# Three early loads on another queue, and the count of rows to redo one row block later

## The chip, the cores and the metric

The kernel runs on one core of a Trainium2 chip. The core has five engines with a queue of their own each: PE (TensorE, matrix products and transposes), DVE (VectorE), ACT (ScalarE), POOL (GpSimd) and SP (SyncE, which issues DMAs). Each queue is worked off in order, and the engines wait for each other through semaphores. The metric is the time of one execution on the device in microseconds.

## The reference, cut to what matters

Two layers on 4096 nodes with 256 features. The first is graph attention with 4 heads, the second a diffusion of two steps, in which a dense attention keeps of each row only the largest probabilities, up to a sum of 0.9.

```python
h = relu(layernorm(x));  x = x + layer0(h, adj, W, a, gamma, beta)
h = relu(layernorm(x));  x = x + layer1(h, adj, W1, W2, W3, U1, U2, ln_g, ln_b)

# layer 0: g = h @ W, 4 heads of 64
src, dst = g . a[:64], g . a[64:]
e = leaky_relu(src[i] + dst[j], 0.2), only where adj[i, j] > 0
out = layernorm(softmax(e) @ g)

# layer 1
R = adj + I, rows divided by their sums
for n in range(2):
    P = softmax((Xa W1^T W2^T)(Xa W3^T)^T)
    A = P, each row cut to its largest entries whose sum reaches 0.9, then rescaled
    Xf = R @ Xf;  Xa = A @ Xa
    Z += Xf @ U1[n]^T + Xa @ U2[n]^T
return layernorm(X + Z)
```

## The kernel before, in words

The 4096 rows are 32 blocks of 128 rows (NB = 32, P = 128); the rows stay in the SBUF tile X. All work stands in stretches under `tc.manual_schedule`: the order of the instructions on each engine is the order in which the program writes them. Loops that would have to be interleaved are written as generators, or as functions that are called between pieces of another loop. DMAs take their semaphores from a set of eight lanes in turn; a DMA that takes a lane again first waits until the one before it on that lane has landed.

The beginning. Block 0 of the rows is loaded by SP (L197), then blocks 1 to 3 in one DMA (L201), then the other 28 blocks in seven DMAs of four blocks (`block_rows`, L195). ACT's queue loads the logits' vector `a_r`, copied to all partitions (L198), the weights in two halves `wx` (L200), and then three small weights of the second layer (L204 to L206). DVE begins with `measured(0)`, the moments of block 0 (L149, L150). Then, for each half k of the weights, it multiplies `wx` with the two halves of `a_r` and adds up (L571, L573, twice each); after k = 0 it takes the moments of blocks 1 to 3, after k = 1 those of blocks 4 to 7. POOL turns moments into scales (`steps`, L141 to L144), ACT normalizes a block (`opened`, L240), PE transposes it (L247) and multiplies it with the weights (L254), and then ACT, DVE and POOL form the weighted rows in three bf16 parts (`turn_of`, once per block). After that PE does the sums over neighbours for 16 passes (L395), and the first hop of the diffusion (L622).

The attention. Step n of the two works through the row blocks b with `attend`. In it there are eight groups g of four columns each: `turn(r, g + 1)` transposes four pieces of the masked exponentials on PE into a PSUM tile `tp` (L1088; there are two such tiles, used in turn) and ACT copies it out to `eT` (L1090); `gather(r, eT[g], g, cur)` multiplies it with the rows (L1096, four matmuls). A dictionary `between` names functions that are called at the end of group g. After the last group come `contributed` (L1106), `weighed` (L1110) and `scaled` (L1101); in the very last block of the last step the first two stand in group 4. `chosen_kept(b)` is DVE's part for a block: it finds the threshold, masks the exponentials (L1022), and carries earlier blocks on through `finish` (L1274 or L1277), `finish_scale` (L1284, L1285), `gathered` (L1114 to L1116), `normal` (L1292), `polished` (L1296 to L1298) and `finish_rows` (L1302 to L1304).

The repair. Rows whose threshold is not certain must be redone. `last_chosen`, called in group 5 of block 30, ends with the tables `undone` and `failed` (`questioned`, L1164 to L1176). `looked`, called in group 6 of block 30, sums them: `counted` calls `totals` twice (PE matmul L878 into a `tp` tile; DVE L880, L882 and L884 read it), and `chosen` makes the list of blocks to redo (DVE, L1192 to L1201). `number` loads the sum into a register of every engine (L1187), and after the last block `repaired` branches on it (L1264). In this run the count is zero and the branch is not taken. In the first step block 31 also prepares the next hop: `both_weights` loads 512 KB of weights (L717), `begin` loads four row blocks and four adjacency rows (L455, L474), `split` and `own` work on these (L461, L462, L482).

Of the kernel before, what the change touches and what calls it, by code (L numbers as in the profile page):

```python
# [26 lines left out]
P = 128  # L27
# [29 lines left out]
def gat_then_top_p_diffusion(  # L57
# [18 lines left out]
    nc = tc.nc  # L76
    N, D = x.shape
    HD = a.shape[0] // 2
    H = D // HD
    DA = w2_t.shape[0]  # L80
    NB = N // P
# [80 lines left out]
    with tc.tile_pool(name="l0", bufs=1) as l0, tc.tile_pool(name="l0s", bufs=2) as l0s, tc.tile_pool(name="l0o", bufs=1) as l0o:  # L162
# [26 lines left out]
        with tc.manual_schedule(engines=every | {ET.SP}):  # L189
            wx = rp.tile([P, KC, D + 2 * H], F32, name="wx", tag="ar", bufs=4)  # L190
            a_r, w1_s, w2_s, w1_r, sT = (rp.tile(sh, F32, name=x, tag="hl", bufs=5) for x, sh in (
                ("a_r", [P, 2 * HD]), ("w1_s", [P, KC, DA]), ("w2_s", [DA, DA]), ("w1_r", [DA, KC, P]), ("sT", [P, P])))
# [2 lines left out]
                nc.sync.dma_start(X[:, ts(g, 4), :], x[ts(g, 4 * P), :].rearrange("(b p) d -> p b d", p=P))  # L195

            nc.sync.dma_start(X[:, 0, :], x[:P, :])  # L197
            nc.scalar.dma_start(a_r, bass.AP(tensor=a.tensor, offset=a.offset, ap=[[0, P], [1, 2 * HD]]))  # L198
            for k in range(KC):
                nc.scalar.dma_start(wx[:, k, :D], w[ts(k, P), :])  # L200
            nc.sync.dma_start(X[:, 1:4, :], x[P:4 * P, :].rearrange("(b p) d -> p b d", p=P))  # L201
            for g in range(1, NB // 4):
                block_rows(g)
# [237 lines left out]
        S = SimpleNamespace(spare=None)  # L441
# [6 lines left out]
        def source(A, n):  # L448
            if n in A.src or n >= len(order):
                return  # L450
            if A.hop == 0:
                A.src[n] = X[:, order[n][1], :]
            else:
                A.src[n] = S.rows.tile([P, D], F32, name="x1", bufs=3) if n % 5 < 3 else S.rows.tile([P, D], F32, name="xa")
                nc.sync.dma_start(A.src[n], xf_d[order[n][1]])  # L455

        def split(A, n):
            while A.parted < min(n, len(order)):
                src = A.src[A.parted]
                hl = rp.tile([P, 2, D], F32R, name="hl", bufs=5)  # L460
                nc.scalar.copy(hl[:, 0, :], src)  # L461
                nc.vector.tensor_tensor(hl[:, 1, :], src, hl[:, 0, :].bitcast(F32), ALU.subtract)  # L462
                A.hl[A.parted] = hl
                A.parted += 1

        def edge(A, n):
            if n in A.ar or n >= len(order):
                return
            p, j = order[n]
            if S.spare is not None and n % 5 == 4:  # L470
                ar = S.spare.tile([P, G0 * P], F32R, name="aru", tag="u")
            else:
                ar = rp.tile([P, G0 * P], F32R, name="ar", bufs=4)
            nc.sync.dma_start(ar.bitcast(F32), adj_d[p, :, j, :].bitcast(F32))  # L474
            A.ar[n] = ar

        def own(A, n):
            while A.owned < min(n, len(order)):
                p, j = order[A.owned]
                if j // G0 == p:  # L480
                    block_ = A.ar[A.owned][:, ts(j % G0, P)]
                    nc.vector.tensor_tensor(block_, block_.bitcast(F32), ident, ALU.add)  # L482
                A.owned += 1
# [171 lines left out]
        def begin(A, n):  # L655
            for i in range(n):
                source(A, i)
                edge(A, i)
            A.begun = n
# [53 lines left out]
    def both_weights():  # L713

        u2 = l1e.tile([P, N + NB], F32, name="u2", tag="e1")[:, :KC * STEPS * D].rearrange("p (k n m) -> p k n m", k=KC, n=STEPS)
        for i in range(STEPS):
            nc.sync.dma_start(u2[:, :, i, :], u2_t[i].rearrange("(k p) m -> p k m", p=P))  # L717
        S.u2 = [u2]
# [150 lines left out]
    def table(name):  # L869
        return small.tile([P, NB], F32, name=name, bufs=1)  # L870

    def col(name, bufs=None):
        return small.tile([P, 1], F32, name=name, bufs=bufs or 4)
# [312 lines left out]
    def number(R, total):  # L1186
        return nc.values_load(total[1], engines=everyone, min_val=0, max_val=6 * P * NB)  # L1187
# [93 lines left out]
    def finish_scale(r):  # L1281
        if r.n + 1 == STEPS:
            r.rs = col("rs")
            nc.gpsimd.tensor_scalar(r.rs, r.mv[:, :, 1], EPS, None, ALU.add)  # L1284
            nc.gpsimd.tensor_tensor(r.rs, r.rs, mhalf, ALU.pow)  # L1285
            if getattr(r, "eased", False):
                r.nmr = col("nmr")
                nc.gpsimd.tensor_scalar(r.nmr, r.mv[:, :, 0], r.rs, -1.0, ALU.mult, ALU.mult)
# [58 lines left out]
    for n in range(STEPS):  # L1347
        cur = X
        G = SimpleNamespace()
        found = [table(f"found{i}") for i in range(3)]  # L1350
        blocks = {}
        with tc.manual_schedule(engines=every):
            pieces = first_hop if n == 0 else hops(second)
            filling, picking = fills(n, G, found, blocks), picks(n, found, blocks)
            done = 0 if n else NB - G0 - LOOK
            for i, _ in enumerate(pieces, 2 * done):
                if n > 0 and i % 6 == 1 and i // 6 < NB // 4:
                    g = i // 6
                    nc.sync.dma_start(cur[:, ts(g, 4), :], xa_d[ts(g, 4)].rearrange("b p d -> p b d"))
                if (n == 0 or i > 10) and i // 2 % NB != NB - 2:  # L1360
                    next(filling, None)
                    if i // 2 % NB < NB - 3 or i % (2 * NB) == 2 * NB - 1:
                        next(picking, None)
                if i == 2 * len(order) - 6:
                    first = turn(blocks[0], 0)
            weights(n)
            for _ in filling:
                next(picking, None)
            for _ in picking:
                pass  # L1370

            def chosen_kept(b):

                r = blocks[b]
                if not hasattr(r, "kept"):
                    candidates(r, found)
                if b > 2:
                    polished(blocks.pop(b - 3))
                if b + 1 < NB and not hasattr(blocks[b + 1], "thirded"):
                    third_probe(blocks[b + 1])  # L1380
                if b > 1:
                    finish(blocks[b - 2])
                    finish_scale(blocks[b - 2])
                if b + 2 < NB and not hasattr(blocks[b + 2], "stepped"):
                    first_step(blocks[b + 2])
                if 0 < b < NB - 1:
                    gathered(blocks[b - 1])
                if not hasattr(r, "kept"):
                    masked(r)
                if 1 < b < NB - 1:  # L1390
                    normal(blocks[b - 2])

            R = SimpleNamespace(n=n, kT=G.kT, qT=G.qT, nm=G.nm, table=found[0])

            def last_chosen():
                chosen_kept(NB - 1)
                R.failed, R.undone = questioned(G, found)

            def looked():
                counted(R)  # L1400
                chosen(R)

            def beginning():
                normal(blocks[NB - 3])
                gathered(blocks[NB - 2])
                finish(blocks[NB - 2])
                finish_scale(blocks[NB - 2])
                R.count = number(R, R.undone)

            beside = {NB - 2: {5: last_chosen, 6: looked}, 0: dict(zip((0, 1, 3, 5, 6), S.turned))}  # L1410
            for b in range(NB - 1):
                chosen_kept(b)
                if b + AHEAD < NB:
                    blocks[b + AHEAD] = began(n, b + AHEAD, G)
                attend(blocks[b], cur, blocks.get(b + AHEAD),
                       beside.get(b, {}), [first] if b == 0 else ())
            r = blocks[NB - 1]

            def earlier():
                polished(blocks[NB - 3])  # L1420
                finish_rows(blocks[NB - 2])

            beside = {0: beginning, 3: earlier}
            if n + 1 < STEPS:
                second = hop_of(n + 1)
                beside.update({1: both_weights, 2: lambda: begin(second, 4), 5: lambda: split(second, 2), 6: lambda: (split(second, 4), own(second, 4))})
            attend(r, cur, None, beside)
            for m in range(second.begun if n + 1 < STEPS else 0):
                for s in range(KC):
                    graph_products(second, m, s, (0,))  # L1430
            finish(r)
            finish_scale(r)
            finish_rows(r)
        repaired(R, cur)
# [32 lines left out]
```

## Time and profile before

| what | value |
|---|---|
| median of 3 runs | 2867.93 us (2864.26 to 2868.86) |
| the profiled execution, its time | 2866.9 us |
| its span in the profile | 2865.1 us |
| TensorE clock granted, mean | 0.995 of full speed |
| PE busy | 2795.3 us, 98% of the span |
| DVE busy | 2169.1 us, 76% |
| ACT busy | 1918.8 us, 67% |
| POOL busy | 865.7 us, 30% |
| the beginning, up to PE's first neighbour sum | some 88 us |
| first step, block 31 and step end | about 1779 to 1811 us |
| last step, block 31 and the end | about 2838 to 2865 us |

Busy time is the time in which an engine had an instruction in work; issuing DMAs and loading registers do not count. The profile shows one execution, so its durations are compared with its own time of 2866.9 us, of which 1.8 us lie outside the span. In a timeline each line gives start and duration in us, the engine, the line of the code, the operation, its output and input, and how many instructions are merged into it; brackets give the time that the engine stood idle before it and what ended that. SPq and ACTq stand for DMA issues of those queues.

### The profile page before, as it was taken

Reading aid. Unit: us, or ns where it says so; the run is one execution under the profiler, and the core shown is the slowest. Engines: PE = TensorE matmul, PEld = TensorE weight load, DVE = VectorE, ACT = ScalarE, POOL = GpSimd, SP = SyncE. Lnnn points to the kernel's source line nnn. Section 1 sums busy time; section 2 is a strip of 40 time slices with the busy share of each in tenths; the row PEclk is TensorE's granted clock in tenths of the full one; section 3 lists DMA queues with packets and bytes.
Section 4 is the critical chain, followed back from the end, with each engine's and each line's share of the span. In section 5 each row is a group of like instructions: output and inputs, shape, how many; then the busy total and the mean of one; then the engine's idle time right before and its main releaser. Section 6 shows DMA issues by size and latency. Waiting matters only on the chain. (4 is left out here: it accounts for less than half of the span.)

```text
span 2865.1 us, 51492 instructions
## 1 busy us (share of the span) xinstructions
PE 2795.3 (98%) x18777; PEld 2436.3 (85%) x18777; DVE 2169.1 (76%) x5069; ACT 1918.8 (67%) x3065; POOL 865.7 (30%) x1811
## 2 busy tenths in 40 slices
PE   5999999999999999999999999999999999999998
PEld 4899999999978788888888888667778888888886
DVE  8867868678554385888888887333665999999996
ACT  7876886879543636788878874233627788777882
POOL 6402121010000121222332231000204756666664
PEclk8999999999999999999999999999999999999999
DMA  8969596696376783000000001767991111111110
GB/s 192 243 250 204 204 234 188 229 198 222 133 236 196 240 298 95 20 20 20 27 20 20 20 20 56 229 200 236 327 340 43 31 41 31 31 31 33 39 29 25
DMA packets 190394, 376.48 MB, mean 131 GB/s; under 512 B 18224, under 2 KB 143152, under 8 KB 186032
## 3 DMA queue, kind: packets, MB, share of 16 engines
q1 hardware_dynamic: 146832, 275.05, 29.9%
q0 software_dynamic: 21504, 83.89, 12.3%
q10 hardware_dynamic: 21792, 14.11, 1.6%
q8 instruction: 152, 2.49, 0.4%
q14 instruction: 114, 0.93, 0.1%
HBM read 305.55 MB, written 113.57 MB: 146 GB/s over the span
## 5 line engine op out<-in xcount | busy, mean ns | idle before, releaser
L1096 PE MATMUL acc<-X,eT 128*128 128x256 f32 x4096 | 973.6, 383 | 3.4 <-ACT eT L1090 2.8
L1096 PEld LDWEIGHTS acc<-X,eT 128*128 128x128 f32 x4096 | 739.1, 190 | 111.5 <-ACT eT L1090 31.5
L395 PE MATMUL acc<-ut,m 128*128 128x195 bf16 (+1 forms) x8192 | 698.7, 246 | 2.2 <-DVE st L412 1.7
L395 PEld LDWEIGHTS <-m 128*128 128x128 fp8e4 x8192 | 695.9, 97 | 4.9 <-DVE st L412 2.2
L369 ACT ACTIVATE g<-sr,d_big 128x1024 uint8<-128x1024 f32 x448 | 472.6, 1136 | 3.4 <-DVE m L375 3.4
L911 ACT ACTIVATE e<-mm,nm 128x1024 f32<-128x1024 f32 x256 | 286.1, 1117 | 200.1 <-PE mm L728 198.8
L1090 ACT COPY eT<-tp 128x512 f32<-128x512 f32 x512 | 296.5, 580 | 87.5 <-PE tp L1088 87.4
L997 DVE MAX8 cand<-big 128x8 f32<-128x228 f32 (+1 forms) x1152 | 348.2, 380 | 0.0
L622 PE MATMUL mm<-ar,hl 128*128 128x512 f32 x844 | 340.7, 407 | 5.9 <-ACT ob L502 1.3
L979 DVE SCALAR_TENSOR_TENSOR big<-e,c 128x4096 f32<-128x4096 f32 x58 | 261.9, 4516 | 97.5 <-POOL c L964 67.1
L622 PE MATMUL acc<-ar,hl 128*128 128x512 f32 x844 | 328.6, 392 | 2.3 <-DVE stage L632 1.3
L935 POOL TENSOR_TENSOR sums<-sums 128x2 f32<-128x2 f32 x64 | 12.6, 197 | 1030.9 <-ACT void L918 1030.9
L1088 PE MATMUL tp<-ident,e 128*128 128x128 f32 x2048 | 306.0, 272 | 0.8 <-DVE e L1022 0.8
L1088 PEld LDWEIGHTS tp<-ident,e 128*128 128x128 f32 x2048 | 254.8, 140 | 60.2 <-PE acc L1106 1.2
L375 DVE TENSOR_TENSOR m<-g,ax 128x512 uint32<-128x512 uint32 x256 | 180.8, 706 | 109.9 <-PE acc L395 91.4
L1022 DVE SCALAR_TENSOR_TENSOR e<-e,found 128x4096 f32<-128x4096 f32 x58 | 259.1, 4468 | 0.0
L918 ACT ACTIVATE void<-e,c1x 128x2048 int8<-128x2048 f32 x128 | 257.4, 2011 | 0.8 <-ACT stage L651 0.8
L918 ACT ACTIVATE void<-e,c 128x2048 int8<-128x2048 f32 x128 | 257.5, 2012 | 0.0
L728 PE MATMUL mm<-kT,qT 128*128 128x512 f32 x512 | 198.4, 468 | 2.9 <-ACT e L911 1.9
L376 DVE TENSOR_TENSOR m<-m,ax 128x512 uint32<-128x512 uint32 x256 | 180.4, 705 | 26.0 <-PE acc L395 0.9
L622 PEld LDWEIGHTS mm<-ar,hl 128*128 128x128 f32 x844 | 158.6, 188 | 44.9 <-issue 5.0
L622 PEld LDWEIGHTS acc<-ar,hl 128*128 128x128 f32 x844 | 158.6, 188 | 39.9 <-issue 4.9
(302 smaller groups left out, 3507.4 us busy)
## 6 DMA issues: line engine op xcount, KB each, us to landing
ar<-adj_d SPq DMA_DIRECT2D x211, 512.0 KB, 4.7
adj_d<-ax POOLq DMA_DIRECT2D x32, 2048.0 KB, 7.7
ut<-uv_d SPq DMA_DIRECT2D x60, 784.0 KB, 5.6
aru<-adj_d SPq DMA_DIRECT2D x45, 512.0 KB, 4.6
ax<-in_adj_t_dram POOLq DMA_DIRECT2D x32, 512.0 KB, 17.4
x<-xf_d SPq DMA_DIRECT2D x78, 128.0 KB, 4.9
xf<-xft_d SPq DMA_DIRECT2D x64, 128.0 KB, 2.3
sr<-s_d SPq DMA_DIRECT2D x15, 512.0 KB, 4.9
```

Source lines behind the costliest of these rows:

```text
L369: nc.scalar.activation(g[:, c, :], shared[k].sr, AF.Relu, scale=BIG, bias=d_big[:, h, j:j + 1])
L395: nc.tensor.matmul(shared[k].acc[i][:, t, :cols], m[t][:, c, ts(i, P)], shared[k].ut[j // QUARTER][:, j % QUARTER, t, :cols], start=(j == ...
L622: nc.tensor.matmul(A.acc[c][s], A.hl[m][:, t, ts(s, P)], A.ar[m][:, ts(c, 512)], start=(j == 0 and t == 0), stop=(j == NB - 1 and t == 1))
L728: nc.tensor.matmul(pm[:, h, :], q[t], kT[:, ds(h * (N // 2) + c * 512, 512)], start=(t == 0), stop=(t == 1))
L911: nc.scalar.activation(ev[:, :, c, :], r.pm[c], AF.Exp, bias=r.nm, accum_out=r.sums[:, c // 2, c % 2:c % 2 + 1])
L918: nc.scalar.activation(void, r.e[:, ts(h, N // 2)], (AF.Relu, AF.Sign)[i], bias=r.c1, scale=-1.0, accum_out=r.sums[:, h, 2 + i:3 + i])
L979: nc.vector.scalar_tensor_tensor(big, r.e, r.c3, r.e, ALU.is_le, ALU.mult, accum_out=r.low3)
L997: nc.vector.max(cand[:, s, :], big[:, edges[s]:edges[s + 1]])
L1022: nc.vector.scalar_tensor_tensor(r.e, r.e, r.t, r.e, ALU.is_ge, ALU.mult, accum_out=kept)
L1088: nc.tensor.transpose(pt[:, i, :], r.e[:, ts(4 * g + i, P)], ident)
L1090: nc.scalar.copy(eT, pt)
L1096: nc.tensor.matmul(r.acc[:, 0, :], eT[:, i, :], cur[:, j, :], start=(j == 0), stop=(j == NB - 1))
```

## The change

The loads of `a_r` and of the two halves of `wx` are issued by SP instead of ACT, at the same place in the program: behind block 0 and ahead of blocks 1 to 3. In the attention, `looked` is called in group 1 of block 31 instead of group 6 of block 30. The load of the count into registers leaves `beginning` (group 0 of block 31) and becomes a function `asked`, called in group 4. In the first step `both_weights` goes from group 1 to group 2, ahead of `begin`. No computation is added or left out.

```diff
             nc.sync.dma_start(X[:, 0, :], x[:P, :])
-            nc.scalar.dma_start(a_r, bass.AP(tensor=a.tensor, offset=a.offset, ap=[[0, P], [1, 2 * HD]]))
+            nc.sync.dma_start(a_r, bass.AP(tensor=a.tensor, offset=a.offset, ap=[[0, P], [1, 2 * HD]]))
             for k in range(KC):
-                nc.scalar.dma_start(wx[:, k, :D], w[ts(k, P), :])
+                nc.sync.dma_start(wx[:, k, :D], w[ts(k, P), :])
             nc.sync.dma_start(X[:, 1:4, :], x[P:4 * P, :].rearrange("(b p) d -> p b d", p=P))
...
                 finish(blocks[NB - 2])
                 finish_scale(blocks[NB - 2])
+
+            def asked():
                 R.count = number(R, R.undone)
 
-            beside = {NB - 2: {5: last_chosen, 6: looked}, 0: dict(zip((0, 1, 3, 5, 6), S.turned))}
+            beside = {NB - 2: {5: last_chosen}, 0: dict(zip((0, 1, 3, 5, 6), S.turned))}
...
-            beside = {0: beginning, 3: earlier}
+            beside = {0: beginning, 1: looked, 3: earlier, 4: asked}
             if n + 1 < STEPS:
                 second = hop_of(n + 1)
-                beside.update({1: both_weights, 2: lambda: begin(second, 4), 5: lambda: split(second, 2), 6: lambda: (split(second, 4), own(second, 4))})
+                beside.update({2: lambda: (both_weights(), begin(second, 4)), 5: lambda: split(second, 2), 6: lambda: (split(second, 4), own(second, 4))})
             attend(r, cur, None, beside)
```

## The prediction

> **What bounds the kernel now.** I read the page first, then the timelines (start, duration, engine, line, operation; in brackets the idle time before it and what ended it) of three stretches that the diff touches: the first 16 us and the last row blocks of the two attention steps.
>
> ```profile
> span 2865.1 us, 51492 instructions
> PE 2795.3 (98%) x18777; PEld 2436.3 (85%) x18777; DVE 2169.1 (76%) x5069; ACT 1918.8 (67%) x3065; POOL 865.7 (30%) x1811
> ```
>
> TensorE is busy 98% of the span, so a gain must be a hole in its time. Where are holes near the change? At the start, before PE has work:
>
> ```profile
> 4.33 0.43 DVE L149 BATCH_NORM_STATS2 st<-X 128x6 f32<-128x256 f32 x1 [4.33 <-DMA X<-in_x_dram]
> 7.69 0.43 DVE L571 TENSOR_TENSOR sr<-wx,a_r 128x256 f32<-128x256 f32 x1 [2.72 <-DMA wx<-in_w_dram]
> ...
> 9.28 0.42 DVE L149 BATCH_NORM_STATS2 st<-X 128x6 f32<-128x256 f32 x1
> ...
> 12.98 0.60 ACT L240 ACTIVATE hb<-X,nmr,rs 128x256 f32<-128x256 f32 x1 [4.14 <-POOL nmr L144]
> ```
>
> DVE works in order: moments of block 0, products with the weights' first half, moments of blocks 1 to 3, products with the second half. It stands 2.72 us for wx; the moments of blocks 1 to 3 (9.28 on) feed POOL's scales, these ACT's second block at 12.98, and that the pipeline. From 20 to 90 us DVE is busy 67.3 of 70 us by the table of windows, so a later start of this pipeline is not made good: it moves everything behind.
>
> The other two holes are at the count. Last step, row blocks 30 and 31:
>
> ```profile
> 2829.65 1.89 PE L1096 MATMUL acc<-X,eT 128*128 128x256 f32 x8
> ...
> 2834.52 0.19 DVE L1176 TENSOR_TENSOR undone<-undone,failed 128x32 f32<-128x32 f32 x1
> ...
> 2834.86 0.27 PE L878 MATMUL tp<-undone,ones 128*1 128x32 f32 x2 [3.32 <-DVE undone L1176]
> ...
> 2835.17 3.44 PE L1096 MATMUL acc<-X,eT 128*128 128x256 f32 x8
> ...
> 2835.51 0.17 DVE L884 CAST ns_i_u<-tp 1x32 int32<-1x32 f32 x1
> ...
> 2854.60 3.62 PE L1096 MATMUL acc<-X,eT 128*128 128x256 f32 x16
> ```
>
> PE is in order; the summing matmul L878 stands in block 30 behind gather 6 and waits 3.32 us for DVE, and gather 7, which needs nothing of it, waits too. That gather then takes 3.44 us where others take 1.89. The same place of the first step:
>
> ```profile
> 1773.44 1.89 PE L1096 MATMUL acc<-X,eT 128*128 128x256 f32 x8
> ...
> 1776.60 0.22 PE L878 MATMUL tp<-undone,ones 128*1 128x32 f32 x2 [1.27 <-DVE undone L1176]
> ...
> 1776.81 1.99 PE L1096 MATMUL acc<-X,eT 128*128 128x256 f32 x8
> ...
> 1777.14 0.17 DVE L884 CAST ns_i_u<-tp 1x32 int32<-1x32 f32 x1
> ```
>
> [...] 3.32 us idle, then 3.44 instead of 1.89; after 1.27 us idle 1.99. [...] wx, issued on ACT at 1.21, and row blocks 1 to 3, issued on SP at 1.19, arrive together (7.69, and 1.19 + 6.6 = 7.79). [...] here L1187 took 0.28 to 0.66.
>
> **The change part by part.** *The count, last step.* Back-to-back gathers are 3.62 - 1.89 = 1.73 us apart, so without L878 gather 7 would start at 2829.65 + 1.73 = 2831.38. It starts at 2835.17, 3.79 later, and is 3.44 - 1.89 = 1.55 longer: 5.34 us leave the path. In the new order L878 stands in block 31 behind gather 1. PE gets there at 2844.80 - 5.34 = 2839.5, and undone is there at 2834.7: no wait. Block 31's transposes move up to 2833.97; its masked rows are ready at 2830.85. What is late next: the two sums sit in the two PSUM tiles "tp", and the transposes of group 3, next on PE, need the first of them back. From L878's start to the end of L884, its last reader, the first step shows 1777.14 + 0.17 - 1776.60 = 0.71 us (0.82 at half clock), plus 0.12 for a handover DVE to PE (1776.45 to 1776.57): 0.83 us given back, L878 itself included. DVE is free for it: ahead of L880 in its queue now stands block 30's finish, which needs POOL's L1116, ACT's L1110 and PE's L1106 (ends at 2839.48 - 5.34 = 2834.14); adding their durations it is over at about 2836.7, 2.8 us early. Net 5.34 - 0.83 = **4.5 us** (3.6 to 4.8).
>
> *The count, first step.* 1773.44 + 1.73 = 1775.17 against 1776.81 is 1.64, and 0.10 from the longer gather: 1.74, less 0.83: **0.9 us** (0.4 to 1.1). It must pass the step's end, where SP's branch and then the loads of adjacency rows lead to PE again at 1811.47; that chain starts from block 31's last matmul, so I let it pass whole.
>
> *What moves along.* The number's load L1187 goes from group 0 to group 4 of block 31 on five queues. PE: at 2840.7 it lay beside gather 0, with no hole after it; 0 to 0.6 us each time, taken as 0. ACT: behind it waits an eT copy, with 2854.60 - 2853.27 = 1.3 us to spare. SP: until now it stood ahead of both_weights' two DMAs and begin's eight (1782.41 to 1788.3); these now go up to 4 us sooner, needed at 1792.5; behind it now is an aru load that waits for PE until 1798.44 anyway. POOL: behind it in step 0 a memset used after 1820, in step 1 L1284, which waits for mv until 2859. DVE: the split L462 at 1792.9, when the number has been there for some 8 us. L1264 needs it only at the end. All at nothing; the price if the cover is gone is the load's 0.3 to 0.66 us. The edits both_weights to group 2 and chosen one block later cost nothing for the same reason.
>
> *The start.* Three DMAs go from ACT to SP between block 0 and blocks 1 to 3. SP issues one per 0.44 us (0.75, 1.19): a_r 1.19, wx 1.63 and 2.08, blocks 1 to 3 at 2.55 instead of 1.19. wx at the earliest 1.63 + 3.6 (block 0's time to land, same size) = 5.2; four DVE operations of 0.42 follow, so moments of block 1 from 6.9 at best. They need blocks 1 to 3: 2.55 + 6.6 = 9.15 with the same time to land, 1.0 more if the 320 KB now ahead of them at 330 GB/s add to it. So between 2.4 us gained and 0.9 lost against 9.28; I take their landing at 8.1, about the middle, because the later rows, which shared the engines, are held back until block 0 has landed (4.33, a semaphore lane of the new order): **1.2 us** gained. ACT no longer waits with its last weight DMA until 7.80, but its first block at 8.24 is not what the second, at 12.98, waits for. Rows 4 to 7 are issued at 4.4 instead of 1.67; read at 12.43, with 7.6 us to land they are there at 12.0, and nearer 9.5 at the rate shown.
>
> *Sum.* 4.5 + 0.9 + 1.2 = 6.6 us. On the profiled execution: 2866.9 - 6.6 = 2860.3 (span 2865.1 to 2858.5). It lies 1.0 below the median of the three runs (2867.93), which scatter over 4.6; on the median **2861.3 us**, -0.23%. About 0.2% (5.7 us, to 2862.2) is what a measurement of this kernel can tell from no change, so I stand close to that line.
>
> **The rivals.** *B: only the end counts.* Blocks 1 to 3 land at 9.2 or later and the start gives nothing, or the step's end takes up the 0.9. For it: their DMA starts 1.36 us later and carries more ahead of it. Against it: DVE's wait names wx alone. 2867.93 - 5.4 = 2862.5; without the first step's part too, 2863.4.
> *C: the sums keep their PSUM tiles.* If the transposes of group 3 are released only at the end of chosen (L1201) and not at L884, PE idles 3.6 us in mid-block (2838.80 - 2835.17)[...]: 0.3 + 3.6 + 0.1 + 1.45 = 5.4 us in each step in place of 0.83. First step 5.4 - 1.74 = +3.7, last +0.1, start -1.2: 2870.5, slower than before; without the start's gain 2871.7. It decides from a wait of some 4 us on. Against it: the last reader of the tile is L884, and L880 starts 0.3 us after L878 in both steps.
> *D: the change doesn't do what it says.* In the changed instruction order L878 does stand behind gather 1 of block 31 and the weights do stand second on SP; I give it no chance of its own.
>
> **How the numbers follow.** Forecast 0.72, B 0.20, C 0.08. The forecast's bounds (3.6 to 4.8, 0.4 to 1.1, 0 to 2.4) with about 1.5 us of scatter leave 0.62 of its 0.72 below 2862.2; B adds 0.04. Faster 0.66; same 0.28 (0.10 + 0.14 + 0.04); slower 0.06 (B 0.02, C 0.04, with a lossy start or a wait above the one assumed). Range 2858.0 (8.3 gained, all parts high, and scatter) to 2866.0 (B with scatter).
>
> **What would show it.** Right: no wait of PE for L1176; the gather after it at 1.89 in block 31; no half clock near the end; 0.4 to 0.7 us idle ahead of the transposes of group 3, ended by DVE; L571 at 5.2 to 6.5, the second L149 near 8.1 and ACT's second block near 11.8. Wrong: that L149 at 9.3 or later (B), a wait of over 3 us ahead of L1088 in block 31 (C), or a span less than 3 us or more than 9 us shorter.

## The result, and the profile after

| | before | after |
|---|---|---|
| median of 11 runs each, us | 2866.23 (2863.07 to 2869.75) | 2859.41 (2856.62 to 2863.27) |
| the profiled execution: time, span, us | 2866.9, 2865.1 | 2858.48, 2856.7 |

The ratio of the runs, after to before, is 0.9979, 95% interval 0.9970 to 0.9987: 6.0 us faster (3.7 to 8.6). The two medians lie 6.8 us apart; 6.6 were forecast. The profiled spans lie 8.4 us apart.

The page of the kernel after, span and busy times:

```profile
span 2856.7 us, 51496 instructions
PE 2793.0 (98%) x18777; PEld 2434.8 (85%) x18777; DVE 2169.4 (76%) x5069; ACT 1919.8 (67%) x3065; POOL 868.3 (30%) x1811
```

PE has as many instructions as before and only 2.3 us less of busy time; most of the 8.4 us are holes that closed.

The start, from the timelines of DVE and ACT after (start, duration, engine, line; in brackets the idle time before and what ended it):

```profile
3.05 0.43 DVE L149 BATCH_NORM_STATS2 st<-X 128x6 f32<-128x256 f32 x1 [3.05 <-DMA X<-in_x_dram]
...
5.95 0.43 DVE L571 TENSOR_TENSOR sr<-wx,a_r 128x256 f32<-128x256 f32 x1 [2.25 <-DMA wx<-in_w_dram]
...
7.56 0.43 DVE L149 BATCH_NORM_STATS2 st<-X 128x6 f32<-128x256 f32 x1
...
11.29 0.60 ACT L240 ACTIVATE hb<-X,nmr,rs 128x256 f32<-128x256 f32 x1 [5.40 <-POOL nmr L144]
```

wx is there 1.74 us sooner (5.95 against 7.69). The moments of block 1 follow at 7.56 with no bracket: blocks 1 to 3 had landed by then, though they were issued later than before, and only wx set the pace. It was close: they were issued at 2.61 and took 4.9 us to land, so they were there at about 7.5, and wx any sooner would have gained next to nothing. ACT's second block comes 1.69 us sooner (11.29 against 12.98). Block 0, which nobody had moved, landed at 3.05 instead of 4.33.

The first step's count, from the timelines of PE and DVE after:

```profile
1771.09 3.62 PE L1096 MATMUL acc<-X,eT 128*128 128x256 f32 x16
...
1780.83 0.22 PE L878 MATMUL tp<-undone,ones 128*1 128x32 f32 x2
...
1781.37 0.17 DVE L884 CAST ns_i_u<-tp 1x32 int32<-1x32 f32 x1
...
1781.59 0.66 PE L1088 MATMUL tp<-ident,e 128*128 128x128 f32 x4 [0.49 <-DVE ns_i_u L884]
```

Gathers 6 and 7 of block 30 are one group of 16 matmuls without a hole. L878 now stands in block 31 and waits for nothing; behind it the transposes wait 0.49 us until DVE has read the sum out of the PSUM tile. The last step's count, the same two engines:

```profile
2810.87 3.65 PE L1096 MATMUL acc<-X,eT 128*128 128x256 f32 x8 [1.04 <-ACT eT L1090]
...
2825.62 3.62 PE L1096 MATMUL acc<-X,eT 128*128 128x256 f32 x16
...
2828.85 0.19 DVE L1176 TENSOR_TENSOR undone<-undone,failed 128x32 f32<-128x32 f32 x1
...
2835.36 0.22 PE L878 MATMUL tp<-undone,ones 128*1 128x32 f32 x2
...
2836.18 0.66 PE L1088 MATMUL tp<-ident,e 128*128 128x128 f32 x4 [0.55 <-DVE ns_i_u L884]
...
2846.20 3.62 PE L1096 MATMUL acc<-X,eT 128*128 128x256 f32 x16
```

The table L1176 is ready 6.3 us before L878 asks for it. But the first line shows something that the profile before did not have at this place: the first gather of block 30 takes 3.65 us, with a granted clock of 0.50 from 2810.83 to 2814.25. Before, behind 1.03 us of idle time, it took 1.99, with a granted clock of 1.00 from 2814.24 to 2817.65:

```profile
2816.55 1.99 PE L1096 MATMUL acc<-X,eT 128*128 128x256 f32 x8 [1.03 <-ACT eT L1090]
```

### The profile page after: what moved, and what is told of

It is laid out like the page before. It is cut to its first block, busy times and chain, and to the rows that moved or that the text cites. A ratio compares the mean times of both kernels' runs of the same rounds, so it can differ in the third digit from the quotient of the medians.

```text
span 2856.7 us, 51496 instructions
## 1 busy us (share of the span) xinstructions
PE 2793.0 (98%) x18777; PEld 2434.8 (85%) x18777; DVE 2169.4 (76%) x5069; ACT 1919.8 (67%) x3065; POOL 868.3 (30%) x1811
## 5 line engine op out<-in xcount | busy, mean ns | idle before, releaser
L1096 PE MATMUL acc<-X,eT 128*128 128x256 f32 x4096 | 973.4, 383 | 3.6 <-ACT eT L1090 3.1
L1096 PEld LDWEIGHTS acc<-X,eT 128*128 128x128 f32 x4096 | 739.3, 190 | 111.9 <-ACT eT L1090 31.9
L935 POOL TENSOR_TENSOR sums<-sums 128x2 f32<-128x2 f32 x64 | 12.9, 202 | 1018.7 <-ACT void L918 1018.7
```

Source lines behind the costliest of these rows:

```text
L1096: nc.tensor.matmul(r.acc[:, 0, :], eT[:, i, :], cur[:, j, :], start=(j == 0), stop=(j == NB - 1))
```

## The experiments

Ratios are to the kernel before, with the runs of before on the same chip (medians 2864.35 for the first four, 2864.07 for the next four, 2866.79 for the last two). "Lead" is how much earlier than in the profile before PE begins a given instruction. Line numbers shift by the lines that an edit adds, so that L1096 can be L1095, L1097 or L1098.

| kernel | median, us | ratio (95%) | in us |
|---|---|---|---|
| e1_start | 2863.06 | 0.9996 (0.9988 to 1.0004) | -1.1 (-3.4 to 1.1) |
| e2_count | 2860.82 | 0.9986 (0.9979 to 0.9992) | -4.0 (-6.0 to -2.3) |
| e3_own | 2857.41 | 0.9976 (0.9968 to 0.9983) | -6.9 (-9.2 to -4.9) |
| e4_busy | 2864.77 | 1.0000 (0.9992 to 1.0009) | 0.0 (-2.3 to 2.6) |
| e5_behind | 2864.49 | 0.9998 (0.9990 to 1.0007) | -0.6 (-2.9 to 2.0) |
| e6_held | 2862.89 | 0.9998 (0.9990 to 1.0006) | -0.6 (-2.9 to 1.7) |
| e7_warm | 2858.25 | 0.9978 (0.9969 to 0.9987) | -6.3 (-8.9 to -3.7) |
| e8_read | 2860.22 | 0.9984 (0.9978 to 0.9991) | -4.6 (-6.3 to -2.6) |
| e9_late | 2873.26 | 1.0021 (1.0013 to 1.0029) | 6.0 (3.7 to 8.3) |
| e10_early | 2877.42 | 1.0033 (1.0021 to 1.0045) | 9.5 (6.0 to 12.9) |

### Each part alone (e1_start, e2_count)

e1 has only the three loads on SP, e2 only the edits in the attention.

> The kernel before with the three loads on SP alone; the count stays where it was. Theory[...]: the products of DVE start near 5.95 us instead of 7.69, the moments of block 1 at about 7.6 instead of 9.28, the first neighbour sum on PE 1.7 to 2.3 us earlier, the span about 2 us shorter (ratio 0.9993), and the wait of 3.3 us in the last step stays. Rival B (blocks 1 to 3 land too late on the one queue): moments of block 1 at 9.2 or later, ratio 1.000.

> The kernel before with the count's move alone; the three loads stay on ACT. Theory: 5.3 us leave the path in the last step and 1.7 in the first, 0.85 to 0.9 comes back in each as a wait of the transposes of group 3; net 5.3 us, ratio about 0.9981. Rival (the gain sits at the end of the first step, where SP's loads went up earlier): PE's lead grows by more than 1 us between block 31's last matmul of the first step and the second hop, and this shows here too. If that growth is only scatter of landing times, it is absent or of either sign here.

e1's start is that of after: L571 at 6.00, the second L149 at 7.59, ACT's second block at 11.32. The lead at the first matmul with the weights is 1.67 us and at the start of the first hop 1.75 (after: 1.70 and 2.20). The size of this gain depends on the profile that it is set against: e2, whose start is that of before, uses wx at 7.00 and e4 at 7.49, where before has 7.69, while the five profiles with the loads ahead on SP lie at 5.87 to 6.09. For ACT's second block it is 12.30 to 12.98 against 11.26 to 11.39, so 0.9 to 1.7 us. The runs give -1.1 us with an interval of 2.2 to each side, so by the runs alone e1 is not told apart from no change. e2 gives 4.0 us. -1.1 and -4.0 add up to -5.1, inside the interval of the whole change. In e2's profile the lead grows by 0.83 us through the first step's count (0.27 to 1.10) and by 2.66 through the last one (0.96 to 3.62), not by the 4.5 forecast there. At the step's end in between it grows by 1.5 us, but so it does in kernels without this edit (see the last point on the prediction). PE of e2 in block 30, first gather:

```profile
2815.62 3.54 PE L1096 MATMUL acc<-X,eT 128*128 128x256 f32 x8 [1.03 <-ACT eT L1090]
```

Again the first gather of block 30 is slow, as in the kernel after (3.54 us here, 3.65 after).

### Is the late start paid in full? (e9_late)

```diff
+            for g in range(1, 6):
+                block_rows(g)
-            nc.scalar.dma_start(a_r, ...)   # and wx[:, 0], wx[:, 1]
+            nc.sync.dma_start(a_r, ...)     # and wx[:, 0], wx[:, 1]
+            for g in range(6, NB // 4):
```

> The kernel before with a_r and the two halves of wx on SP behind 24 blocks of rows, so 3 MB later in the queue: a test, enlarged, of the step that a later start of the pipeline is not made good. Theory: at 330 GB/s 3 MB take some 9.5 us, L571 begins at 10.5 to 13 us instead of 7.69, ACT's second block comes as much later, and the time grows by about the same 3 to 5 us: ratio to before 1.0010 to 1.0018. Rival (the neighbour stage or a later one takes the delay up, so that the start's 1.7 us were worth nothing): the delay is gone by the first neighbour sum or by the first hop, ratio 0.9996 to 1.0006.

DVE, first products of the weights and then ACT's second block, e9:

```profile
14.21 0.43 DVE L573 TENSOR_TENSOR sr<-wx,a_r 128x256 f32<-128x256 f32 x1 [10.62 <-DMA wx<-in_w_dram]
...
19.51 0.60 ACT L242 ACTIVATE hb<-X,nmr,rs 128x256 f32<-128x256 f32 x1 [13.74 <-POOL nmr L144]
```

The 330 GB/s are what the DMAs of the profile before moved from 8 to 10 us (332 and 329), but the estimate of the landing was too early: wx comes 6.52 us later than before, not 3 to 5. What the run was made for holds: ACT's second block is 6.53 us later, the first neighbour sum 6.28, the first hop 6.27, the second step's block 27 6.51, and the runs 6.0 (3.7 to 8.3). No stage makes this late start good, and the rival falls. An earlier start is kept in the profiles too: the five with the loads ahead on SP lead by 1.59 to 1.73 us at the first matmul with the weights and, but for e7 (0.87), by 1.74 to 2.20 at the first hop. The runs of e1 are too coarse to tell.

### Why wx comes sooner (e5_behind, e6_held)

e5: the three loads on SP but behind blocks 1 to 3. e6: the weights left on ACT, and the later rows held until block 0 has landed.

```diff
# e6_held, the only edit
+            nc.vector.tensor_copy(X[:, 4, :1], X[:, 0, :1])
             for g in range(1, NB // 4):
                 block_rows(g)
```

> The kernel before with a_r and the two halves of wx on SP, but behind row blocks 1 to 3 instead of ahead of them; rows 4 and on wait for block 0, as in the changed kernel. Theory (order on the one queue decides[...]): wx lands after blocks 1 to 3, so DVE's L571 begins at 7.2 to 8.2 us, right before it no hole is saved, ACT's second block comes at 12.6 to 13.5 and the time is that of before within 0.1%. Rival (what helps is that rows 4 to 7 and 8 to 11 no longer share the DMA engines with the weights): L571 at 6.5 or earlier, ACT's second block at 11.8 or earlier, 1.0 to 1.7 us faster.

> The kernel before (weights on ACT) with one added DVE copy of one column, X[:, 0, :1] to X[:, 4, :1] ahead of the loads of rows 4 and on, so that these are issued only once block 0 has landed; the column is overwritten by the load. Theory (order on one queue): the weights still share the engines with blocks 1 to 3, L571 at 7.0 to 7.8 us and ACT's second block at 12.3 to 13.1, gain below 0.7 us. Rival (fewer transfers at once): L571 at 6.5 or earlier and ACT's second block at 11.8 or earlier, 1.0 to 1.7 us faster. Block 0 itself, which landed at 4.33 before and at 3.05 after: if it comes at 3.1 here, the rows behind it had slowed it.

DVE's first products in e5, then block 0 (read by the added copy L202) and the first products (here L572) in e6:

```profile
7.11 0.43 DVE L571 TENSOR_TENSOR sr<-wx,a_r 128x256 f32<-128x256 f32 x1 [3.32 <-DMA wx<-in_w_dram]
```

```profile
4.97 0.15 DVE L202 COPY X<-X 128x1 f32<-128x1 f32 x1 [4.97 <-DMA X<-in_x_dram]
...
6.65 0.42 DVE L572 TENSOR_TENSOR sr<-wx,a_r 128x256 f32<-128x256 f32 x1 [0.98 <-DMA wx<-in_w_dram]
```

In the profile before, the two queues do share the DMA engines: from 4 to 8 us SP's DMAs took 77.3% and ACT's 23.2% of the time of the 16 engines. But neither theory has it alone. wx is used at 7.69 in before (7.00 to 7.69 in the profiles with its order), 7.11 in e5, 6.65 in e6 and 5.95 in after. The change also holds the later rows back, unasked: SP issues their first three DMAs at 3.09, 5.31 and 5.87 instead of 1.67, 2.19 and 5.48, because three more DMAs stand ahead of them in its queue and the second of the three then waits 1.7 us for the lane of `a_r`. e6 shows that holding them helps by itself (0.35 us sooner than the soonest of the old order, 1.04 sooner than before), but it holds them longer than the change does, until 5.15. e5 has the later rows and the queue about as after, with blocks 1 to 3 ahead of the weights, and lies within the old order's range. From e5 to e1, which differ in this order alone, wx comes 1.11 us sooner (7.11 to 6.00). So the place ahead of blocks 1 to 3 is the largest step seen; how the whole divides into order and hold is not shown.

ACT's second block follows: 12.41 in e5, 11.95 in e6. Both missed their range at the near end (e6 below 7.0, e5 just below 7.2), and in the runs neither can be told from no change. e6's lead of 1.04 at the first matmul with the weights is 0.64 at the first hop, e5's 0.57 is 0.82. What takes 0.4 us of e6's lead in between was not shown.

Block 0: 3.14 in e5, where blocks 1 to 3 were issued right behind it on the same queue, 4.97 in e6, where the rows of blocks 4 and on were held. So it was not the later rows that had delayed it, but `a_r` and wx on the other queue.

### What the count's wait costs (e4_busy, e10_early)

e4 keeps the count where it was and fills PE's wait: 30 transposes into a spare PSUM tile ahead of the sums in the last step, 12 in the first, with nothing left out. e10 calls `looked` in group 5 of block 30, one group earlier than before.

```diff
# e4_busy, in counted
+        idle = bank()
+        for i in range(15 if R.n + 1 == STEPS else 6):
+            for k in range(KC):
+                nc.tensor.transpose(idle[:, ts(k, P)], X[:, 0, ts(k, P)], ident)
# e10_early
-            beside = {NB - 2: {5: last_chosen, 6: looked}, ...
+            beside = {NB - 2: {5: lambda: (last_chosen(), looked())}, ...
```

> The kernel before with transposes of a row block into a free PSUM tile, read by nobody, ahead of the count's sums: 30 of them in the last step (some 3.2 us, the length of the wait), 12 in the first (1.3 us). The wait for DVE stays as long as it was, but PE isn't idle in it. Theory (half clock after the idle 3.3 us): the gather behind it takes 1.9 to 2.0 us instead of 3.44, no half clock near the end, the span about 1.5 us shorter, ratio 0.9995. Rival (the gather was slow for another reason, such as its operands): it stays at 3.4 us and the time at 1.000.

> The kernel before with the count one group earlier instead of nine pieces later: the summing matmuls stand ahead of gather 6 of block 30 instead of behind it. Theory (each us that PE waits for the table at the count is paid in full[...]): the wait grows by one group of transposes and gather, 0.44 + 1.73 = 2.17 us, to 3.4 us in the first step and 5.5 in the last; in the first step half clock follows, 1.5 us more; and the sums' tiles hold the transposes of group 7 up by 0.5 us in both. First step +4.2, last +2.7, together 6.9 us slower, ratio 1.0024 (1.0015 to 1.0030). Rival (a wait of PE at the count is mostly made good behind it, where PE waits for other engines anyway): below 2 us slower, ratio below 1.0007.

PE of e4 in the last step, the filling and the gather behind the sums:

```profile
2830.79 3.44 PE L1183 MATMUL mm<-ident,X 128*128 128x128 f32 x30
...
2834.49 1.99 PE L1096 MATMUL acc<-X,eT 128*128 128x256 f32 x8
```

The gather takes 1.99 us instead of 3.44, and in this stretch the profile gains 1.55 us. This is not proof that the filling did it, since e5 has 1.99 there behind 3.32 us of wait that nothing filled. The runs show nothing of it (0.0, -2.3 to 2.6), so whether the typical execution gains stays open in e4. The waits of e10, PE, first step and then last step:

```profile
1777.34 0.22 PE L878 MATMUL tp<-undone,ones 128*1 128x32 f32 x2 [3.46 <-DVE undone L1176]
...
1778.59 5.30 PE L1096 MATMUL acc<-X,eT 128*128 128x256 f32 x16
```

```profile
2823.25 3.41 PE L1096 MATMUL acc<-X,eT 128*128 128x256 f32 x8 [1.04 <-ACT eT L1090]
...
2841.54 0.27 PE L878 MATMUL tp<-undone,ones 128*1 128x32 f32 x2 [3.79 <-DVE undone L1176]
...
2843.32 5.72 PE L1096 MATMUL acc<-X,eT 128*128 128x256 f32 x16
```

In the first step the wait is 3.46 (3.4 expected), the two gathers behind it take 5.30 instead of 3.62, and PE loses 4.38 us (it is 0.71 behind the profile before ahead of this place and 5.09 after it; 4.2 expected). The wait for the table is paid in full, and 1.68 us of slower gathers come on top of it. In the last step 5.5 were expected and 3.79 came, because the first gather of block 30 had already been slow (3.41): PE was 1.7 us later at the count, and the table came when it came. The gathers behind the count were slow again (5.72 instead of 3.62), and in all PE loses 3.7 us here, where 2.7 were expected. The runs lost 9.5 us (6.0 to 12.9), which leaves room for the 6.9. This profile also loses 2.6 us in the second hop, which the edit does not touch; why was not shown.

### Where the half clock falls

All profiles in which the count stands as before and its wait is not filled, gathers and wait in us:

| kernel | first gather of block 30 | wait for L1176 | gather behind the count |
|---|---|---|---|
| before | 1.99 | 3.32 | 3.44 |
| e1_start | 1.99 | 3.31 | 3.78 |
| e9_late | 1.99 | 3.31 | 3.78 |
| e5_behind | 1.99 | 3.32 | 1.99 |
| e6_held | 3.43 | 1.64 | 1.99 |

The e6 row, PE in the last step:

```profile
2813.44 3.43 PE L1097 MATMUL acc<-X,eT 128*128 128x256 f32 x8 [1.03 <-ACT eT L1091]
...
2831.74 0.22 PE L879 MATMUL tp<-undone,ones 128*1 128x32 f32 x2 [1.64 <-DVE undone L1177]
```

With the count ahead of gather 7, PE starts that gather when the table is there, whatever happened earlier in the block: in e6 the 1.44 us that the first gather takes longer (3.43 against 1.99) are swallowed by a shorter wait (1.64 against 3.32). A slow gather costs extra only where it falls behind the count (before, e1, e9: 3.44 to 3.78). With the count moved off, nothing swallows it: of the profiles without the wait, after, e2 and e8 have the slow gather in block 30 (3.65, 3.54, 3.54), e3 does not (1.99).

Why it comes in one execution and not in the next was not shown. The length of a wait alone does not decide it: behind 3.31 and 3.32 us at the count the gather was slow in before, e1 and e9 and not in e5. The traces of before and after also show the granted clock. In both, each period of half clock ahead of the one that runs into the end lasts 3.41 or 6.83 us, so that stretches of 3.41 us show what PE did ahead of one. A line gives start and end of a stretch, its length, busy times (PE's first), and as the third number from the end the granted clock. Block 30 of the last step, after and then before:

```profile
2807.42:2810.83 3.41, 1.57 (x11) 0.96 (x9) 3.38 (x11) 1.56 (x4) 3.22 (x5) 1.00 0.00 0
2810.83:2814.25 3.42, 3.38 (x8) 2.75 (x9) 3.42 (x14) 0.48 (x1) 2.34 (x4) 0.50 0.03 10
```

```profile
2810.83:2814.24 3.41, 2.83 (x14) 2.14 (x12) 3.41 (x2) 0.47 (x1) 3.41 (x1) 1.00 0.01 2
2814.24:2817.65 3.41, 2.16 (x13) 1.85 (x14) 3.38 (x14) 1.56 (x3) 3.22 (x7) 1.00 0.00 0
```

The wait at the count, before:

```profile
2831.31:2834.72 3.41, 0.23 (x2) 0.00 (x0) 3.06 (x12) 0.00 (x0) 1.92 (x4) 1.00 0.00 0
2834.72:2838.13 3.41, 3.27 (x11) 2.65 (x12) 2.56 (x19) 0.00 (x0) 0.00 (x0) 0.50 0.00 0
```

In after, block 30's two waits (0.84 and 1.04 us) fall almost whole into the stretch ahead of the half clock, and PE works 1.57 us in it; in before they fall into two stretches, with 2.83 and 2.16 us of work, and the clock stays at 1.00. Ahead of the half clock behind before's count PE works 0.23 us. But PE's work in the stretch ahead does not decide it alone either: 1.44 us (after, 2848.38 to 2851.79) and 1.94 us (before, 83.57 to 86.99) were followed by a clock of 1.00, and 2.11 us (before, 42.61 to 46.03) by 0.50.

### Filling block 30's waits (e7_warm)

e7 is e3 (below) with eight transposes of X into a spare PSUM tile ahead of block 30's first transposes in the last step, and eight ahead of its first gather.

```diff
+        if warm:                          # last step, block NB - 2
+            spare()                       # 8 transposes into bank()
         eT = list(eT) or [turn(r, 0)]
...
+            if warm and g == 0:
+                spare()
             gather(r, eT[g], g, cur)
```

> The kernel with both sums in one PSUM tile of their own (e3), with 8 matmuls more (transposes of X into a spare PSUM tile) ahead of the first transposes of row block 30 in the last step and 8 more ahead of its first gather, where PE stood 0.8 and 1.0 us. Theory (those two waits together draw the half clock there[...]): no half clock near the end, the first gather of block 30 at 1.89 to 1.99 us instead of 3.65, the two waits gone or below 0.2 us; in the median of the runs 0 to 1.5 us faster than e3, so a ratio to before of 0.9970 to 0.9976. Rival (the half clock comes from elsewhere, such as the work before): the gather at 3.4 or more in spite of it. Second rival (the added matmuls delay the path): the gathers start 0.5 to 1.5 us later, ratio 0.9980 or above.

```profile
2808.51 1.04 PE L1136 MATMUL mm<-ident,X 128*128 128x128 f32 x8
...
2810.36 1.04 PE L1136 MATMUL mm<-ident,X 128*128 128x128 f32 x8
2811.56 1.99 PE L1095 MATMUL acc<-X,eT 128*128 128x256 f32 x8 [0.16 <-ACT eT L1089]
```

PE in block 30: the waits are filled, 0.16 us is left, and the gather takes 1.99 us, no later than without. But e3's own profile had 1.99 there too, so this profile does not show that the filling prevented anything in it. The runs (0.9978) cannot be told from e3 (0.9976). What the filling would save on average stays open; e3's interval leaves room for it.

### The PSUM tiles of the two sums (e3_own)

e3 is the changed kernel with both sums in one tile of the other PSUM pool, so that the two `tp` tiles stay with the transposes.

```diff
-    def totals(t, name):
+    def totals(t, name, pn):
-        pn = ps2.tile([P, 4, P], F32, name="tp")[:, 0, :]
...
+        both = ps2.tile([P, 2, 512], F32, name="mm")
-        R.undone, R.failed = totals(R.undone, "u"), totals(R.failed, "f")
+        R.undone, R.failed = totals(R.undone, "u", both[:, 0, :]), totals(R.failed, "f", both[:, 1, :])
```

> The changed kernel, with both sums of the count in one PSUM tile of the other kind (mm), which is free in block 31, instead of two of the transposes' tiles. Theory (the transposes of group 3 wait for their tile): their wait of 0.5 to 0.6 us goes in both steps, PE's two sums stay with some 0.2 to 0.3 us; about 1.2 us less than the changed kernel, ratio to before about 0.9975. Rival (they wait for something else that DVE does at that time): the wait stays and the time is that of the changed kernel.

PE of e3 in block 31 of the last step, the sum and the transposes of group 3:

```profile
2834.68 0.22 PE L877 MATMUL mm<-undone,ones 128*1 128x32 f32 x2
...
2834.89 0.66 PE L1087 MATMUL tp<-ident,e 128*128 128x128 f32 x4
```

The bracket of 0.55 us is gone. The lead falls by 0.36 us in both steps, in place of the 0.91 and 0.97 of the kernel after; what is left is L877 itself and a slightly longer transposing. That names the wait after the change: the tiles. In the runs e3 is the fastest of all, but by less than the intervals; against the kernel after it is not decided.

### Reading the number (e8_read)

```diff
-            beside = {0: beginning, 1: looked, 3: earlier, 4: asked}
+            beside = {0: beginning, 1: lambda: (looked(), asked()), 3: earlier}
```

> The changed kernel with the count's number read by all five engines right behind the count (group 1 of block 31) instead of three groups further on. Theory (the read is a register load that PE and ACT can't begin before the count is cast, so that reading it further on is what makes it free): PE stands 0.3 to 0.9 us more ahead of the transposes of group 3 in each step, 0.6 to 1.8 us slower than the changed kernel in all, ratio to before about 0.9982 to 0.9985. Rival (the load lies beside the sums' wait that is there anyway): no more idle than the 0.5 us that PE has there in the changed kernel, ratio about 0.9979.

PE, transposes behind the sums, first step and last step of e8:

```profile
1782.37 0.63 PE L1088 MATMUL tp<-ident,e 128*128 128x128 f32 x4 [0.92 <-DVE ns_i_f L884]
```

```profile
2841.20 0.63 PE L1088 MATMUL tp<-ident,e 128*128 128x128 f32 x4 [0.81 <-DVE n_i_f L882]
```

0.92 instead of 0.49 and 0.81 instead of 0.55: the early read costs 0.43 and 0.26 us, at the low end of the theory's 0.3 to 0.9 and, in the last step, just below it; the rival, no more idle time, falls. The ratio (0.9984) agrees with the theory, but its interval holds both. In the kernel after, three groups further on, PE has no hole at the load.

## Why the prediction was right, point by point

- *The total.* 6.6 forecast; 6.8 by the medians, 6.0 by the ratio (3.7 to 8.6). The median is 1.9 us below the 2861.3 given, since the runs of before, with eight more, came out 1.7 lower too. The sum was nearer than its terms, which is partly luck: in the profile after, the three terms come to 5.2 us (last point).
- *The count, first step: right.* The lead grows by 1.75 us and falls by 0.91 (1.74 and 0.83 forecast), net 0.84. That it passes the step's end whole is not shown: the profiles agree with it, since no lead is lost there, but they scatter by more than the 0.84.
- *The count, last step: the wait right, the half clock mis-sized.* From the second gather of block 30 to the end of gather 7 the lead grew by 5.3 us, as worked out, and 0.97 were given back for 0.83. But the 1.55 us of half clock in that sum were booked as belonging to the wait: the author's estimate, from 3.32 us idle with 3.44 behind it and 1.27 idle with 1.99 behind it. In the profile after, half clock (a granted clock of 0.50) came in block 30, behind waits of 0.84 and 1.04 us, and took 1.66 back, against the sign "no half clock near the end": net 2.7 us through this step (lead 5.73 to 8.40) instead of 4.5. e3, without it, shows 5.36 gained and 0.36 given back. So 4.5 was the term's best case. In an execution like e5's or e6's the count costs the kernel before only the 3.79 of the wait; set against an execution of the kernel after that has the half clock, 3.79 - 1.66 - 0.97 = 1.2 us are left. What decides which of these comes, and how often each occurs, single profiles do not tell.
- *What is late next: right.* The transposes of group 3 wait for the sums' tile, 0.49 and 0.55 us, ended by DVE's L884; rival C, a hold until the end of `chosen` with a slow gather behind it (an estimate: 1.45 us, the 3.44 less the 1.99 of the profile before), is out. e3 shows that it is the tile.
- *The start: right, with one landing mis-sized.* 1.2 forecast; 1.7 against the profile before, 0.9 to 1.7 over all profiles with the old and the new order. The step that was off is the landing of blocks 1 to 3, taken as 8.1 from the middle of two bounds: both bounds kept the 6.6 us to land of before, and it took 4.9. They were there at about 7.5 and held nobody up, so wx was the limit. wx itself came 0.75 later than its earliest estimate, 5.2. That the later rows are held back was named as a reason; e6 shows that it helps, but not how much of the gain is due to it. That a later start is not made good was an argument from a table of busy times; e9 shows it for a start 6.5 us later. Rival B's late landing falls with the 7.56.
- *The number's load, both_weights and chosen: at nothing, right.* No new hole stands at any of them; e8 gives the price of the other order, 0.26 to 0.43 us a step.
- *The profile's 8.4 us.* Start 1.7, first step 0.84, last step 2.7 are 5.2. Another 0.6 arises between the start and the first count and 1.1 in the second hop, which the change does not touch; in the second hop the other profiles differ among each other by more (from 0.9 gained to 2.6 lost). And 1.5 lies at the first step's end, where SP takes 2.94 us from the last store (L1275) to the first load (L455) instead of 4.60. This is not the change: e1, e4, e5 and e6, which keep the count as before, make up 1.1 to 1.8 us against the profile before at the same place. The profile before was a slow one there. The part that the runs show and these terms do not (5.2 against 6.0) is inside the interval.

## What to carry to other kernels

An engine that works in order pays for a wait with everything queued behind it (gather 7, which needs nothing of the count, started 3.79 us late), so a small reduction belongs where its input has long been ready (6.3 us in the kernel after), and its output tile should not be one that the main stream needs next (0.49 and 0.55 us, gone in e3). When a wait goes, ask what it used to absorb: in e6 the count's wait swallowed a slow first gather of the block (1.64 us of wait instead of 3.32), and in the profile after, without the wait, 1.66 us of it are paid. When a DMA landed depended here on what stood ahead of it in its queue (wx used at 6.00 us ahead of blocks 1 to 3, at 7.11 behind them) and on the loads of the other queue (block 0 at 4.33 and 3.05), and three more DMAs in a queue held back one that follows by a semaphore lane (rows issued at 5.31 instead of 2.19), for good or ill.

## What the runs showed of the hardware that was not expected

- The first gather of block 30 took 3.41 to 3.65 us in five profiles (after, e2, e6, e8, e10) and 1.99 in six (before, e1, e3, e4, e5, e9), behind the same idle times in both (0.79 to 0.84 and 1.03 to 1.04 us, with 1.06 or 1.07 us of work between). In after the granted clock was 0.50 there, in before 1.00. And at the count 3.32 us of idle time were followed by a gather of 1.99 us in e5, of 3.44 in before.
- Loads on a second queue delayed one that had been issued first on its own: block 0 (128 KB, issued at 0.75) was first used at 4.33 (before) and 4.97 us (e6) with `a_r` and wx (320 KB) on ACT's queue, and between 2.95 and 3.14 (after, e1, e5, e9) with them on SP's, even with blocks 1 to 3 right behind it on the same queue (e5, e9). With the small weights (144 KB) on ACT's queue from 0.77 on it was 3.05 (after); with the first of them issued at 5.18 it was 2.95 (e9).
